# An attention kernel's products with v: six key tiles at a time, after two turns of scores in a row

## The chip, the cores and the metric

The kernel runs on one core of a Trainium2 chip. The metric is the device time of one execution in microseconds (us). Three executions of the kernel before took 3902.34, 3902.94 and 3906.36 us; their median, 3902.94 us, is the time before. The profiled execution has a span of 3893.8 us, and times read from the profile refer to that span.

## The reference

The kernel computes four layers one after the other on an image of 48 x 48 positions with 768 channels: a vision-transformer block, a Fourier mixing layer, a scan with a small convolution, and a second Fourier layer. The change touches only the attention inside the first layer. Cut to that part:

```python
# 12 heads of 64 channels, 2304 tokens (48 x 48)
attn = einsum('bqc,bkc->bqk', q * scale, k)
rel_h = einsum('bhwc,hkc->bhwk', r_q, Rh)     # position terms, per query
rel_w = einsum('bhwc,wkc->bhwk', r_q, Rw)
attn = softmax(attn + rel_h + rel_w, axis=-1)
out = einsum('bqk,bkc->bqc', attn, v)
```

All data is f32, except that the position terms are held in bf16.

## The kernel before, in words

The stages follow each other: layer norm with the q, k and v projections, attention, the output projection, the two layers of the MLP, then the other three layers. Attention is `attention_bounded` (L523). It works on pairs of heads: six pairs (`pr`), each with its 2 x 64 channels on the 128 partitions. The queries are cut into six chunks of 384 (`qc`), the keys into 18 tiles of 128 (`kt`). Scores are held with the keys on the partitions and the queries along the row, so that the product with v needs no transpose. Since the scores are known to be bounded, the exponential is taken with no maximum subtracted, and the sum over the keys is divided out at the end.

For one key tile there are four steps:

- `products` (L551): for each of the two heads one f32 matmul, keys times queries, 64 rows deep. The two heads use the upper and the lower half of the array's rows. The result fills a two-bank tile `s` in PSUM; the pool `at_ps` has three of them[...].
- `scores` (L559): for each head a bf16 matmul with a one-hot matrix (L564) adds the position terms to the same tile. ScalarE then takes the exponential of both heads at once (L566) into a tile `p` of SBUF from the pool `at_p`, and VectorE adds `p` to the running sum `acc` (L571, L574).
- `values` (L578): for each head one f32 matmul (L585), v times `p`, with 64 result rows. The two heads use the left and the right half of the array's columns, and add up over all 18 key tiles in one PSUM tile `av`.
- at the end of a chunk `row_sums` (L587) adds `acc` over the partitions with two matmuls (L592) and takes the reciprocal, and `finish` (L597) multiplies.

The loop at L604 runs over 216 turns (`work`, 36 chunks of six turns); a turn is `KB` = 3 key tiles of one chunk. In turn i the loop writes down `products` for its three tiles, then `scores` for them, and then `values` for the three tiles of the turn before. So a product with v never waits for its own exponentials: those of a turn run while TensorE does the products with v of the turn before it.

This is the order in which the program is written; a scheduler then gives each engine its own order. It takes instructions by priority, which is the order of writing, but may take a later one first where it reckons that the earlier one is not ready. Each engine works through its own list in order.

Beside attention, `weight_sums` (L735) prepares sums of weight blocks for later stages on GpSimd. It is advanced by one step every seven turns (L605), and takes the tiles through which it loads from the same pool `at_p` as the exponentials (L603).

Of the kernel before, what the change touches and what calls it, by code (L numbers as in the profile page):

```python
# [522 lines left out]
def attention_bounded(tc, ahead, oT, beside):  # L523

    nc = tc.nc
    QB = TB
    KB = 3
    (load_keys_values, load_chunk), kvs, qbs, ones, oneh = ahead
    with (
        tc.tile_pool(name="at_p", bufs=10) as pp,  # L540
        tc.tile_pool(name="at_r", bufs=2) as rp,
        tc.tile_pool(name="at_o", bufs=2) as op,
        tc.tile_pool(name="at_ps", bufs=3, space=PSUM) as ps_s,
        tc.tile_pool(name="at_pv", bufs=1, space=PSUM) as ps_v,
    ):
        keys = [kv[:, :T] for kv in kvs]
        vals = [kv[:, T:].rearrange("p (t c) -> p t c", t=NT) for kv in kvs]

        probs, scs = {}, {}

        def products(c, kt):  # L551
            pr, qc = c
            ps = ps_s.tile([P, 2, 512], F32, tag="s", name=f"s_{pr}_{qc}_{kt}")
            for s in range(2):
                rows = slice(s * HD, (s + 1) * HD)
                nc.tensor.matmul(ps[:, s, :QB], lhsT=keys[pr % 2][rows, kt * P : (kt + 1) * P], rhs=qbs[qc % 2][0][rows], start=True, stop=False)  # L556
            scs[c, kt] = ps

        def scores(c, kt):  # L559
            pr, qc = c  # L560
            b, j = divmod(kt, KJ)
            ps = scs.pop((c, kt))
            for s in range(2):
                nc.tensor.matmul(ps[:, s, :QB], lhsT=oneh[:NBR, b % 3, :], rhs=qbs[qc % 2][1][:NBR, s, b // 3, j, :], start=False, stop=True)  # L564
            p = pp.tile([P, 2, QB], F32, tag="p", name=f"p_{pr}_{qc}_{kt}")
            nc.scalar.activation(p, ps[:, :, :QB], AF.Exp)  # L566
            probs[c, kt] = p

            if kt == 1:
                acc = rp.tile([P, 2, QB], F32, tag="acc", name=f"acc_{pr}_{qc}")  # L570
                nc.vector.tensor_tensor(acc, probs[c, 0], p, ALU.add)  # L571
                probs[c] = acc
            elif kt > 1:
                nc.vector.tensor_tensor(probs[c], probs[c], p, ALU.add)  # L574

        avs, recs = {}, {}

        def values(c, kt):  # L578
            pr, qc = c
            if kt == 0:  # L580
                avs[c] = ps_v.tile([P, 512], F32, tag="av", name=f"av_{pr}_{qc}")
            p = probs.pop((c, kt))
            for s in range(2):
                rows = slice(s * HD, (s + 1) * HD)
                nc.tensor.matmul(avs[c][rows, :QB], lhsT=vals[pr % 2][:, kt, rows], rhs=p[:, s, :], start=kt == 0, stop=kt == NT - 1)  # L585

        def row_sums(c):  # L587
            pr, qc = c
            acc = probs.pop(c)
            rs = ps_v.tile([P, 512], F32, tag="rs", name=f"rs_{pr}_{qc}")  # L590
            for s in range(2):
                nc.tensor.matmul(rs[s * HD : (s + 1) * HD, :QB], lhsT=ones, rhs=acc[:, s, :], start=True, stop=True)  # L592
            rec = rp.tile([P, QB], F32, tag="rec", name=f"rec_{pr}_{qc}")
            nc.vector.reciprocal(rec, rs[:, :QB])
            recs[c] = rec

        def finish(c):  # L597
            pr, qc = c
            av, rec = avs.pop(c), recs.pop(c)
            nc.vector.tensor_tensor(oT[:, pr, qc * QB : (qc + 1) * QB], av[:, :QB], rec, ALU.mult)  # L600

        work = [((pr, qc), k0) for pr in range(NC) for qc in range(T // QB) for k0 in range(0, NT, KB)]
        other = beside(op, lambda name: pp.tile([P, 2, QB], F32, tag="p", name=name))  # L603
        for i in range(len(work) + 1):  # L604
            if i % 7 == 3:  # L605
                next(other, None)
            if i < len(work):
                c, k0 = work[i]
                pr, qc = c
                if k0 == 0:  # L610
                    nxt = (pr, qc + 1) if qc + 1 < T // QB else (pr + 1, 0)
                    if nxt[0] < NC:
                        load_chunk(qbs[nxt[1] % 2], nxt)
                    if qc == 1 and pr + 1 < NC:
                        load_keys_values(kvs[(pr + 1) % 2], pr + 1)
                for kt in range(k0, k0 + KB):
                    products(c, kt)
                for kt in range(k0, k0 + KB):
                    scores(c, kt)
            if i:  # L620
                c, k0 = work[i - 1]
                if k0 + KB == NT:
                    row_sums(c)
                for kt in range(k0, k0 + KB):
                    values(c, kt)
                if k0 + KB == NT:
                    finish(c)
        for _ in other:
            pass
# [627 lines left out]
def block_kernel(ctx: ExitStack, tc: tile.TileContext, a: dict):  # L1257
# [52 lines left out]
    with tc.If(bounded > 0) as which:  # L1310
        attention_bounded(tc, ahead, oT, beside)
# [387 lines left out]
```

## Time and profile before

| what | value |
|---|---|
| time, median of three | 3902.94 us |
| span of the profiled execution | 3893.8 us |
| TensorE matmul (PE) busy | 3755.5 us, 96% |
| TensorE weight loads (PEld) busy | 2283.2 us, 59% |
| VectorE (DVE) busy | 2050.0 us, 53% |
| ScalarE (ACT) busy | 1141.6 us, 29% |
| GpSimd (POOL) busy | 654.2 us, 17% |
| attention, first to last of its matmuls | 513.5 to 1690.1 us |
| in it: PE, DVE, ACT, POOL busy | 1171.5, 718.0, 480.1, 140.4 us |

PE stands for the matmuls and PEld for the weight loads, which overlap with them. Matmuls are pipelined: each is shown for about 0.48 us, while the next may start after 0.32 us. So a single duration of PE says little, and the distance between starts, or the busy time of a group divided by its count, says what one costs. In a line of the groups the fields are: source line, engine, operation, what it writes and reads, shapes, count; then the busy time of the group in us and the mean of one in ns; then the idle time of the engine just before the group's instructions, and what ended it. In a line of the timeline they are: start in us, length in us, engine, source line, operation, shapes and how many follow each other, and in brackets the idle time before.

In attention the granted clock of TensorE is 1.00 throughout.

### The profile page before, as it was taken

The page shows a single profiled execution, that of the slowest core. Times are in us where ns is not written, and L with a number is a line of the kernel's source. Part 1 is how long each engine was busy: PE and PEld are TensorE (multiplying, and loading weights), DVE is VectorE, ACT ScalarE, POOL GpSimd, SP SyncE. Part 2 cuts the span into 40 slices and gives each one's busy share as a digit, 9 for nine tenths or more (in the row PEclk, how much of TensorE's full clock was granted, in tenths as well). Part 3 has the DMA queues.
Part 4 walks back from the last instruction along what each step waited for, and adds up shares of the span by engine and source line. Part 5 has one row for each costly group of instructions (what it writes and reads, how often), then busy time and mean ns, then how long its engine had stood idle before and what let it go on. Part 6 is the DMA issues. An engine that isn't in the chain of part 4 may idle for free.

```text
span 3893.8 us, 54463 instructions
## 1 busy us (share of the span) xinstructions
PE 3755.5 (96%) x22018; PEld 2283.2 (59%) x22018; DVE 2050.0 (53%) x3185; ACT 1141.6 (29%) x1907; POOL 654.2 (17%) x496
## 2 busy tenths in 40 slices
PE   8999989999999999989999999999979998999998
PEld 4666544444444444445555555555558876996685
DVE  6655456666666666545425233232335358995445
ACT  1322244444444444411310120021013246223341
POOL 3101011111111111024000000000023210981131
PEclk9999999999999999999999999999989789999999
DMA  7656563424232322134335434533443312110434
GB/s 256 212 186 199 177 182 95 132 88 131 96 98 89 98 89 73 30 114 161 118 106 161 151 102 123 155 111 109 142 116 98 95 36 96 35 37 23 145 98 167
DMA packets 266954, 460.43 MB, mean 118 GB/s; under 512 B 33005, under 2 KB 219365, under 8 KB 260327
## 3 DMA queue, kind: packets, MB, share of 16 engines
q1 hardware_dynamic: 257063, 436.23, 36.4%
q10 hardware_dynamic: 9632, 20.65, 1.4%
q8 instruction: 175, 2.87, 0.3%
q14 instruction: 84, 0.69, 0.1%
HBM read 318.49 MB, written 138.31 MB: 117 GB/s over the span
## 4 chain that ended last, share of the span: by engine, by line
PE 87%; DVE 5%; DMA 4%; ACT 2%; issue 1%; SPq 1%; POOL 1%; ACTq 0%; DVEq 0%; POOLq 0%
PE p L860 13%; PE p L923 13%; PE s L556 11%; PE av L585 11%; PE qk L294 6%; PE s L564 6%; PE c L1076 4%; PE v L163 3%; PE pj L163 2%; PE f_z L1447 2%; PE f_z L1448 2%; PE f_x L1412 2%; PE f_u L1462 2%; PE so L1237 2%; PE f_w L1549 2%; DVE s L1186 2%
## 5 line engine op out<-in xcount | busy, mean ns | idle before, releaser
L574 DVE TENSOR_TENSOR acc<-acc,p 128x768 f32<-128x768 f32 x576 | 581.8, 1010 | 354.1 <-ACT p L566 315.9
L566 ACT ACTIVATE p<-s 128x768 f32<-128x768 f32 x648 | 478.4, 811 | 688.7 <-PE s L564 578.9
L923 PE MATMUL p<-w,h 128*128 128x384 f32 x1512 | 492.7, 486 | 0.0
L556 PE MATMUL s<-qt,kv 64*128 64x384 f32 x2592 | 477.7, 501 | 8.4 <-ACT p L566 4.7
L585 PE MATMUL av<-p,kv 128*64 128x384 f32 x2592 | 464.5, 493 | 0.0
L923 PEld LDWEIGHTS p<-w,h 128*128 128x128 f32 x1512 | 286.3, 190 | 196.7
L556 PEld LDWEIGHTS s<-qt,kv 64*128 64x128 f32 x2592 | 232.7, 186 | 248.8 <-ACT p L566 113.8
L585 PEld LDWEIGHTS av<-p,kv 128*64 128x64 f32 x2592 | 170.0, 136 | 225.2 <-issue 215.9
L860 PE MATMUL p<-x2nT,w 128*128 128x384 f32 x864 | 293.2, 489 | 3.9 <-POOL rr L899 3.9
L294 PE MATMUL qk<-xnT,wqk 128*128 128x384 f32 x756 | 251.5, 489 | 5.6 <-DMA wqk<-wqk_d 5.6
L1166 PE MATMUL c<-H,bands 128*48 128x96 f32 x5632 | 242.1, 247 | 11.7 <-issue 11.5
L564 PE MATMUL s<-bt,oneh 120*128 120x384 bf16 x1296 | 248.8, 328 | 0.0
L1166 PEld LDWEIGHTS c<-H,bands 128*48 128x48 f32 x5632 | 234.1, 123 | 19.8 <-issue 11.9
L860 PEld LDWEIGHTS p<-x2nT,w 128*128 128x128 f32 x864 | 165.2, 191 | 119.4 <-POOL rr L899 4.1
L860 PE MATMUL p<-xT,w 128*128 128x384 f32 x648 | 220.8, 486 | 0.0
L564 PEld LDWEIGHTS <-oneh 120*128 120x128 bf16 x1296 | 109.3, 98 | 174.5 <-issue 115.4
L294 PEld LDWEIGHTS qk<-xnT,wqk 128*128 128x128 f32 x756 | 144.2, 192 | 99.7 <-issue 7.9
L899 POOL TENSOR_TENSOR rr<-rr,ml_b 128x1152 f32<-128x1152 f32 x12 | 32.1, 2675 | 955.0 <-DMA rr<-xr_d 861.6
L855 ACT ACTIVATE h<-h,ml_b 128x384 f32<-128x384 f32 x144 | 88.3, 614 | 345.9 <-DVE h L875 174.3
L1174 POOL TENSOR_TENSOR t<-s,c 128x768 f32<-128x768 f32 x80 | 144.7, 1835 | 171.9 <-DVE s L1136 160.8
L860 PEld LDWEIGHTS p<-xT,w 128*128 128x128 f32 x648 | 123.2, 190 | 85.8
L1076 PE MATMUL c<-wsc,x2T 128*112 128x357 f32 (+1 forms) x576 | 151.6, 426 | 2.0 <-DVE c L1037 2.0
(312 smaller groups left out, 4763.5 us busy)
## 6 DMA issues: line engine op xcount, KB each, us to landing
w<-w1s_d SPq DMA_DIRECT2D x36, 768.0 KB
w<-w2s_d SPq DMA_DIRECT2D x36, 768.0 KB
bt<-rh_d SPq DMA_DIRECT2D x144, 162.0 KB
w<-w1s_d SPq DMA_DIRECT2D x36, 576.0 KB
w<-in_mlp_w_dram SPq DMA_DIRECT2D x27, 768.0 KB
wqk<-wqk_d SPq DMA_DIRECT2D x12, 1344.0 KB
yu<-f_ys SPq DMA_DIRECT2D x24, 672.0 KB
f_gt<-yu SPq DMA_DIRECT2D x24, 672.0 KB
```

Of the source, the lines that this page charges most:

```text
L163: nc.tensor.matmul(p[:, :TB], lhsT=rhs[n][:, c, t * P : (t + 1) * P], rhs=w[:, c, :], start=c == 0, stop=c == NC2 - 1)
L294: nc.tensor.matmul(p[:, :TB], lhsT=w[:, n, c, :], rhs=ops[sb][n][:, c, :], start=c == 0, stop=c == NC2 - 1)
L556: nc.tensor.matmul(ps[:, s, :QB], lhsT=keys[pr % 2][rows, kt * P : (kt + 1) * P], rhs=qbs[qc % 2][0][rows], start=True, stop=False)
L564: nc.tensor.matmul(ps[:, s, :QB], lhsT=oneh[:NBR, b % 3, :], rhs=qbs[qc % 2][1][:NBR, s, b // 3, j, :], start=False, stop=True)
L566: nc.scalar.activation(p, ps[:, :, :QB], AF.Exp)
L574: nc.vector.tensor_tensor(probs[c], probs[c], p, ALU.add)
L585: nc.tensor.matmul(avs[c][rows, :QB], lhsT=vals[pr % 2][:, kt, rows], rhs=p[:, s, :], start=kt == 0, stop=kt == NT - 1)
L860: nc.tensor.matmul(p[:, :TB], lhsT=w[n][:, c, :], rhs=rhs[n][:, c, :], start=c == 0, stop=c == NC2 - 1)
L923: nc.tensor.matmul(ps[t][:, :TB], lhsT=hs[left, f][:, t * P : (t + 1) * P], rhs=wt[:, f % KW2, :], start=f == 0, stop=f == NF2 - 1)
L1076: nc.tensor.matmul(ps[:K, i, :n], lhsT=xT[:, cc, tok : tok + K], rhs=w[:, cc, c0 : c0 + n], start=cc == 0, stop=cc == NC - 1)
L1166: nc.tensor.matmul(ps[r0 : r0 + G, k // 4, cols], lhsT=bands[:, n - GC, i, :] if gr else bands0[:, n, i, :], rhs=H[:, n, :, d : d + NPR], ...
L1174: GP.tensor_tensor(t, sc[:, ch], c1[:, m0 : m0 + GC].unsqueeze(2).to_broadcast([P, GC, RR, NPR]), ALU.mult)
```

## The change

The products with v are no longer written after every turn, but after every second one, and then for the six key tiles of the two turns before. Two turns of `products` and `scores` so follow each other with no `values` written between them. Since the number of turns in a chunk is even, a burst of six always belongs to one chunk. More tiles of exponentials are then alive at once, up to nine instead of six, so the pool `at_p` gets 13 buffers instead of 10. The purpose is that TensorE passes less often from one kind of product to another. What is computed, and the number of every kind of instruction, stay the same.

```diff
@@ attention_bounded
-        tc.tile_pool(name="at_p", bufs=10) as pp,
+        tc.tile_pool(name="at_p", bufs=13) as pp,
...
-            if i:
+            if i and i % 2 == 0:
                 c, k0 = work[i - 1]
                 if k0 + KB == NT:
                     row_sums(c)
-                for kt in range(k0, k0 + KB):
+                for kt in range(k0 - KB, k0 + KB):
                     values(c, kt)
                 if k0 + KB == NT:
                     finish(c)
```

## The prediction

> **What bounds the kernel now.** I began with the page's busy shares: PE 96% of the span, the next engine 53%. The chain of work that ended last says the same, and says how much of it is the attention this change touches:
>
> ```profile
> PE 87%; DVE 5%; DMA 4%; ACT 2%; issue 1%; SPq 1%; POOL 1%; ACTq 0%; DVEq 0%; POOLq 0%
> ```
>
> Its line for attention (L556, L564, L585) gives 11%, 6% and 11% of 3893.8 us. So I went to the groups of instructions, where the product lines stand with their counts, and a full-array line for comparison:
>
> ```profile
> L574 DVE TENSOR_TENSOR acc<-acc,p 128x768 f32<-128x768 f32 x576 | 581.8, 1010 | 354.1 <-ACT p L566 315.9
> L566 ACT ACTIVATE p<-s 128x768 f32<-128x768 f32 x648 | 478.4, 811 | 688.7 <-PE s L564 578.9
> L923 PE MATMUL p<-w,h 128*128 128x384 f32 x1512 | 492.7, 486 | 0.0
> L556 PE MATMUL s<-qt,kv 64*128 64x384 f32 x2592 | 477.7, 501 | 8.4 <-ACT p L566 4.7
> L585 PE MATMUL av<-p,kv 128*64 128x384 f32 x2592 | 464.5, 493 | 0.0
> L564 PE MATMUL s<-bt,oneh 120*128 120x384 bf16 x1296 | 248.8, 328 | 0.0
> ```
>
> Two readings. PE loses 8.4 us to waits in the whole attention; ACT and DVE wait for PE and not the reverse. And the busy time divided by the count: L585 464.5/2592 = 179 ns a pass, while L923, which fills the array, takes 492.7/1512 = 326 ns for the same 384 columns of f32. An f32 product is two passes (2592 passes for 1296 products), and the two heads' passes of L585 run side by side on the two column halves. A lone pass costs 326 ns, not 179.
>
> One turn (three key tiles) in order of time, PE alone:
>
> ```profile
> 902.15 2.21 PE L556 MATMUL s<-qt,kv 64*128 64x384 f32 x12
> 904.29 1.15 PE L564 MATMUL s<-bt,oneh 120*128 120x384 bf16 x6
> 905.37 2.16 PE L585 MATMUL av<-p,kv 128*64 128x384 f32 x12
> 907.46 0.92 PE L556 MATMUL s<-qt,kv 64*128 64x384 f32 x4
> ```
>
> Starts give the turn: products with k 2.14, bias 1.08, products with v 2.09, together 5.31 us. 216 turns x 5.3 us, plus 36 row sums of 0.70, are 1170 of the attention's 1177 us (513.5 to 1690.1). The weight loads of the same burst show its rhythm:
>
> ```profile
> 905.37 0.20 PEld L585 LDWEIGHTS av<-p,kv 128*64 128x64 f32 x4 [0.32 <-issue]
> 905.75 0.14 PEld L585 LDWEIGHTS av<-p,kv 128*64 128x64 f32 x2 [0.18 <-issue]
> 906.07 0.14 PEld L585 LDWEIGHTS av<-p,kv 128*64 128x64 f32 x2 [0.18 <-issue]
> 906.39 0.14 PEld L585 LDWEIGHTS av<-p,kv 128*64 128x64 f32 x2 [0.18 <-issue]
> 906.72 0.14 PEld L585 LDWEIGHTS av<-p,kv 128*64 128x64 f32 x2 [0.18 <-issue]
> ```
>
> Loads come two at a time, one per head, each 0.322 us after the last. A burst of six products is six such slots: 6 x 0.3225 = 1.935 us, and the other 0.15 of its 2.09 us is the switch: about 0.05 for the first weight load and 0.10 for the change to the next kind of product.
>
> **What the Trainium skill says.** "TensorEngine Tiling (Array Packing)", Key Properties: changing the tiling mode drains TensorE, while different tiles load and multiply in parallel. The trace agrees with both (0.15 us a burst; two loads per slot). "TensorE: Matmul & The Clock Gate", What overlaps and what doesn't: matmuls start and end strictly in program order. So a product with v that stands ahead of the next products with k is not overtaken; no trace here contradicts it. The same page, Measured speedup vs the span model, gives a packed group the time of one matmul plus about 4 ns a tile; here the slot of a pair equals L923's lone slot (0.32 us), so splitting a pair makes two slots of one.
>
> **What the change does to the order.** From the source I would expect, per two turns, k-products and bias twice and then twelve products with v. The built program differs, and its order on PE is what the chip runs. With P for products with k, S for bias, V for products with v, each with its number of products, it reads (steady state; row sums left out):
>
> ```
> before: P6 S6 V6    P6 S6 V6
> after:  P6 S6 V1    P6 S6 V11
> ```
>
> 107 times the scheduler puts one product (head 0 of the burst's first tile) between the two turns, and the burst starts with head 1 of that tile. Sums agree: 107 x 12 plus 12 in the last bursts = 1296 = 2592/2.
>
> **Part by part.**
> (1) Kinds of product change as often as before: six switches per two turns in both orders. The saving that a burst of six tiles could bring is therefore zero.
> (2) V1 has no partner. Its two passes take two slots alone: 2 x 0.3225 = 0.645 us plus its switch. V11 holds head 0 of five tiles and head 1 of six, so head 1's half sets its length: 6 x 2 = 12 slots, the same as twelve paired products. Per two turns V slots go from 12 to 14: +0.645 us, all on the path, since PE has nothing idle to put it in. 107 x 0.645 = +69.0 us. Lower bound: V1 with one weight load spared the 0.05 us of the first load, 0.593 x 107 = 63.5. Upper bound: a lone slot at the 326 ns of L923 and another 0.05 us of switch, about 0.70 x 107 = 75. I take 69, since the first pass waits for its weights either way.
> (3) The new wait: the second turn's P needs the score buffers (three) that the first turn's exponentials read. In the trace the exponentials begin at 904.83, 2.68 us after P starts, and are 0.70 apart:
>
> ```profile
> 904.83 2.21 ACT L566 ACTIVATE p<-s 128x768 f32<-128x768 f32 x3 [3.09 <-PE s L564]
> ```
>
> They end 3.49, 4.19 and 4.89 us after that P. The second P starts at 2.14 + 1.08 + 0.79 (V1 and its switch) = 4.01; its three tiles start two slots apart, with 0.1 us more after the first weight load: 4.01, 4.76 and 5.40. Each finds its buffer free by 0.5 us, so the wait costs nothing; behind it would stand S, V11 and all of PE, so 0.1 us of it would be 11 us in all.
> (4) ACT has 2.21 and DVE 3.08 us of work per turn (three exponentials; three sums). The shorter gap between turns is now 4.0 us, so neither becomes the bound. Row sums, where a chunk ends, come after the second turn's bias, at 4.01 + 2.14 + 1.08 = 7.23; the last of the sums they read (begun about 0.8 us behind the exponentials, 3.08 long) ends near 6.7: hidden.
> (5) Buffers 10 to 13: nine tiles of exponentials are alive instead of six, so four stay for the weight sums beside attention, as before. That sharing costs one stall in the trace:
>
> ```profile
> 548.99 2.21 ACT L566 ACTIVATE p<-s 128x768 f32<-128x768 f32 x3 [8.14 <-POOL pw0p L130]
> 549.85 1.62 PE L556 MATMUL s<-qt,kv 64*128 64x384 f32 x8 [3.21 <-ACT p L566]
> ```
>
> With 13 buffers that slot is first reused one turn later (the first exponential of the second chunk), over 5 us after; POOL is done by then. -3.2 us.
> (6) SyncE's queue moves a few weight loads behind bias loads; both are prefetched a chunk or more ahead (32 us), nothing.
> Sum: 3902.9 + 69.0 - 3.2 = 3968.7 us.
>
> **Rivals.**
> A, the lone product is free: its slots fall into time that the array loses anyway. Then only (5) is left, 3899.7; and if a V switch went as well (0.15 x 107 = 16) 3884. For it: the loader is idle 0.32 us ahead of each burst. Against: that gap is half of V1's slots, and the switch is not removed. Chance 0.06.
> B, the order as in the source: one switch less per two turns (-16), but the second P would come at 3.22 and wait for the first exponential until 3.49 plus about 0.05 for the signal: 0.32 x 107 = +34. 3902.9 - 16 + 34 - 3 = 3918. Against: the built order. Chance 0.04.
> C, V11 does not pair: every burst before starts with head 0, this one with head 1. If its 11 products ran singly, 22 slots instead of 12: 3.2 us x 107 more, 4314. For it: no trace has such a burst. Against: pairing here looks like two halves that each work off their own products. Chance 0.05.
>
> **How the numbers follow.** Main case 0.85: 3968.7, from 3963 to 3975 by the bounds of (2). The range widens these by ten-odd us for a stall that comes back (3.2 us each) or 0.1 us of the wait in (3): 3951 to 3987. A, B and C stay outside it. Faster by over 0.2% is the further half of A and a margin, 0.05; same 0.03; slower 0.92.
>
> **What would show it.** Right: attention (first L556 to last L585) longer by 62 to 72 us and everything after it unchanged; L585's busy time up by about 69 us with 2592 passes still; between two turns a group of L585 x2 of about 0.8 us, then a group of x22 of about 4.0; L556 still with a few us of idle on ACT. Wrong: L556 idle on exponentials of tens of us (B), an L585 group of x22 lasting 7 us (C), or groups of x2 that don't lengthen the two turns beyond 10.6 us (A).

## The result, and the profile after

| | before | changed |
|---|---|---|
| time, median | 3903.28 us | 3964.84 us |
| span of the profiled execution | 3893.8 us | 3964.2 us |
| attention, first to last of its matmuls | 1176.6 us | 1239.3 us (514.4 to 1753.7) |
| PE busy in the span | 3755.5 us | 3827.0 us |

The changed kernel is slower: the ratio is 1.0158, with a 95% interval from 1.0141 to 1.0176. In the two profiled executions attention takes 62.7 us more, and the medians of the time differ by 61.6 us. The spans of the profiled executions differ by 70.4 us; most of the rest, 6.9 us, lies after attention (2203.7 and 2210.6 us). In the nine traces of this document that stretch, which no edit touches, lasts between 2201 and 2212 us, so this is scatter and not the change.

The chain of work that ended last, by engine:

```profile
PE 89%; DVE 4%; DMA 3%; ACT 1%; issue 1%; POOL 0%; SPq 0%; ACTq 0%; DVEq 0%; POOLq 0%
```

PE's share rises from 87% to 89%; what came on top lies on PE. The groups of instructions that answer to those shown of before (after the bar: busy us, mean ns, idle before):

```profile
L574 DVE TENSOR_TENSOR acc<-acc,p 128x768 f32<-128x768 f32 x576 | 576.3, 1001 | 448.3 <-ACT p L566 409.6
L566 ACT ACTIVATE p<-s 128x768 f32<-128x768 f32 x648 | 478.5, 811 | 752.7 <-PE s L564 676.6
L585 PE MATMUL av<-p,kv 128*64 128x384 f32 x2592 | 532.4, 491 | 0.0
L923 PE MATMUL p<-w,h 128*128 128x384 f32 x1512 | 492.7, 486 | 0.0
L556 PE MATMUL s<-qt,kv 64*128 64x384 f32 x2592 | 476.5, 500 | 5.2 <-DVE rest_w L371 3.4
L564 PE MATMUL s<-bt,oneh 120*128 120x384 bf16 x1296 | 248.2, 328 | 0.0
```

Of the groups on PE shown here, the products with v (L585) are the only one that grew: 532.4 us busy instead of 464.5, with the same 2592 passes, nearly the same mean duration (491 and 493 ns) and no idle time before them. The others are as they were, to about 1 us. A group that costs 68 us more with equal instructions and no wait is one whose instructions overlap less.

The same stretch of two turns on PE, from the timeline:

```profile
908.80 2.21 PE L556 MATMUL s<-qt,kv 64*128 64x384 f32 x12
910.94 1.15 PE L564 MATMUL s<-bt,oneh 120*128 120x384 bf16 x6
912.02 0.86 PE L585 MATMUL av<-p,kv 128*64 128x384 f32 x2
912.81 2.21 PE L556 MATMUL s<-qt,kv 64*128 64x384 f32 x12
914.95 1.15 PE L564 MATMUL s<-bt,oneh 120*128 120x384 bf16 x6
916.03 4.08 PE L585 MATMUL av<-p,kv 128*64 128x384 f32 x22
920.04 0.59 PE L556 MATMUL s<-qt,kv 64*128 64x384 f32 x2
```

The two passes of the lone product (x2) hold the array from 912.02 to 912.81, 0.79 us, and the burst of 22 passes takes 4.01 us, which is what 24 passes in pairs would take. Two turns last 920.04 - 908.80 = 11.24 us instead of 10.61, which is twice the 5.303 us of the kernel before. Each kind of work on PE goes straight into the next; no bracket with an idle time stands at any of these lines.

### The profile page after: what moved, and what is told of

It reads as the page before. It is cut to its first block, busy times and chain, and to the rows that moved or that the text cites. A ratio compares the mean times of both kernels' runs of the same rounds, so it can differ in the third digit from the quotient of the medians.

```text
span 3964.2 us, 54473 instructions
## 1 busy us (share of the span) xinstructions
PE 3827.0 (97%) x22018; PEld 2315.1 (58%) x22018; DVE 2050.4 (52%) x3185; ACT 1141.9 (29%) x1907; POOL 645.3 (16%) x496
## 4 chain that ended last, share of the span: by engine, by line
PE 89%; DVE 4%; DMA 3%; ACT 1%; issue 1%; POOL 0%; SPq 0%; ACTq 0%; DVEq 0%; POOLq 0%
PE av L585 13%; PE p L860 12%; PE p L923 12%; PE s L556 12%; PE s L564 6%; PE qk L294 6%; PE c L1076 4%; PE pj L163 3%; PE v L163 3%; PE f_x L1412 2%; PE f_z L1447 2%; PE f_z L1448 2%; PE f_u L1462 2%; PE so L1237 2%; PE c L1166 2%; PE f_w L1549 2%
## 5 line engine op out<-in xcount | busy, mean ns | idle before, releaser
L585 PE MATMUL av<-p,kv 128*64 128x384 f32 x2592 | 532.4, 491 | 0.0
L556 PE MATMUL s<-qt,kv 64*128 64x384 f32 x2592 | 476.5, 500 | 5.2 <-DVE rest_w L371 3.4
L556 PEld LDWEIGHTS s<-qt,kv 64*128 64x128 f32 x2592 | 232.3, 186 | 245.2 <-issue 67.6
L585 PEld LDWEIGHTS av<-p,kv 128*64 128x64 f32 x2592 | 198.7, 137 | 264.3 <-issue 264.2
```

## The experiments

The first four were timed beside the same runs of the kernel before, the last three beside another set of such runs. Line numbers shift by one or more where an edit adds lines; the tile names show what a line is. In the diffs `last[0]` is the last bias matmul written so far, and `tc.issue_after` keeps TensorE's work in its block behind it; `values` takes the heads to do where only one is meant. P, S and V are used as in the prediction.

### One part alone: 13 buffers

```diff
-        tc.tile_pool(name="at_p", bufs=10) as pp,
+        tc.tile_pool(name="at_p", bufs=13) as pp,
```

> The kernel before with 13 buffers of exponentials and nothing else changed. Theory (buffers only remove the one stall on a weight-sum tile near the start): the 3.2 us of PE idle before the products with k at 549.85 are gone, attention 1173.4 us instead of 1176.6, time 3900.0 us. Rival (more buffers let the scheduler or the queues move something that costs): 3905 us or more.

Measured: 3898.53 us, ratio 0.9984 (0.9976 to 0.9992), attention 1172.9 us. The group of products with k, in the lines of attention alone:

```profile
L556 PE MATMUL s<-qt,kv 64*128 64x384 f32 x2592 | 477.8, 501 | 5.0 <-DVE rest_w L371 3.4 <-ACT p L566 1.6
```

The idle time before L556 falls from 8.4 to 5.0 us. What follows: the larger pool costs nothing and takes away one stall. The loss must lie in the new order.

### The same two turns with a pair ahead instead of a lone product

Against the changed kernel: the burst's first key tile is written after the odd turns, both heads, and held behind the last bias product, so that the scheduler cannot take half of it:

```diff
-            if i and i % 2 == 0:
+            if i % 2:
+                c, k0 = work[i - 1]
+                with tc.issue_after(last[0].ins):
+                    values(c, k0)
+            elif i:
                 c, k0 = work[i - 1]
                 if k0 + KB == NT:
                     row_sums(c)
-                for kt in range(k0 - KB, k0 + KB):
-                    values(c, kt)
+                with tc.issue_after(last[0].ins):
+                    for kt in range(k0 - KB + 1, k0 + KB):
+                        values(c, kt)
```

> The changed kernel with both heads of the burst's first key tile between the two turns instead of one: P6 S6 V2 P6 S6 V10. The number of switches and the early start of the burst are the same as in the changed kernel; only the pairing of that tile's two products differs. Theory (the cost is the missing partner): V slots per two turns 2 + 10 = 12 as before, time 3900 us (before, less the stall), attention 1173 us. Rival (the cost is that the burst is taken apart, whatever stands in front): time stays at 3940 to 3965 us.

Measured: 3899.65 us, ratio 0.9987 (0.9981 to 0.9994), attention 1174.6 us. On PE:

```profile
914.52 1.15 PE L565 MATMUL s<-bt,oneh 120*128 120x384 bf16 x6
915.60 0.87 PE L586 MATMUL av<-p,kv 128*64 128x384 f32 x4
916.40 2.21 PE L557 MATMUL s<-qt,kv 64*128 64x384 f32 x12
918.53 1.15 PE L565 MATMUL s<-bt,oneh 120*128 120x384 bf16 x6
```

The visit of four passes lasts 915.60 to 916.40, 0.80 us: the same as the changed kernel's visit of two passes (0.79). The second head's product came along for nothing, and the burst behind it shrank from 4.01 to 3.38 us. (3.38 us is the median of its 107 bursts.) One product moved by one place is worth about 65 us. This is the comparison that settles the cause: order of visits, number of switches and buffers are those of the changed kernel. The hold behind the bias products, which is new here, is no rival: the next kernel has it too, and there the cost is larger and not gone.

### Two lone products

Against the changed kernel: head 0 of the burst's first two key tiles stands between the turns; in the burst, head 1 of these is then set beside head 0 of the tiles two further on, so that all that can pair does:

```diff
+            if i % 2:
+                c, k0 = work[i - 1]
+                with tc.issue_after(last[0].ins):
+                    for kt in range(k0, k0 + 2):
+                        values(c, kt, (0,))
...
-                for kt in range(k0 - KB, k0 + KB):
-                    values(c, kt)
+                with tc.issue_after(last[0].ins):
+                    for n in range(2 * KB):
+                        values(c, k0 - KB + n, (1,))
+                        if n + 2 < 2 * KB:
+                            values(c, k0 - KB + n + 2, (0,))
```

> The changed kernel with two lone products between the two turns, head 0 of the burst's first two key tiles; the burst then takes head 1 of these tiles paired with head 0 of later ones: four pairs and two lone products of head 1. Theory (each lone product costs the slots in which it has no partner): V slots per two turns 4 + 12 = 16 instead of 14 in the changed kernel and 12 before, 0.645 us more each, 107 times: 69 us over the changed kernel, 4034 us. Rival (the cost belongs to the visit, not to the number of lone products): 3965 us.

Measured: 4038.74 us, ratio 1.0337 (1.0320 to 1.0354), attention 1310.1 us, 70.8 us over the changed kernel. On PE:

```profile
911.29 1.50 PE L586 MATMUL av<-p,kv 128*64 128x384 f32 x4
912.73 2.21 PE L557 MATMUL s<-qt,kv 64*128 64x384 f32 x12
```

Four passes as with the pair ahead, but all of one head: 911.29 to 912.73, 1.44 us instead of 0.80. Each further lone product costs its two slots, and the visit as such nothing more.

### The order as written: nothing between the two turns

Against the changed kernel, the whole burst is held behind the second turn's bias products:

```diff
-                for kt in range(k0 - KB, k0 + KB):
-                    values(c, kt)
+                with tc.issue_after(last[0].ins):
+                    for kt in range(k0 - KB, k0 + KB):
+                        values(c, kt)
```

> The changed kernel with the products with v of a burst held behind the last bias product written before them, so that no lone product stands between the two turns: P6 S6 P6 S6 V12. Theory (the lone product costs two unpaired slots, 0.645 us each time): these 69 us go; one switch less per two turns saves 0.15 x 107 = 16 us; the second turn's products with k now wait about 0.32 us for the first exponential, 34 us in all. Time about 3918 us, attention about 1191 us, V22 and V2 groups replaced by V24 of 4.02 us, L556 idle on ACT about 35 us. Rival (long bursts as such are slow, or holding more exponentials is): time stays near 3965 us. Rival (the wait is larger than thought, the second and third tile wait too): 3940 us or more with over 55 us of idle on ACT.

Measured: 3935.65 us, ratio 1.0071 (1.0054 to 1.0088), attention 1211.0 us. On PE:

```profile
906.56 2.21 PE L557 MATMUL s<-qt,kv 64*128 64x384 f32 x12
908.70 1.15 PE L565 MATMUL s<-bt,oneh 120*128 120x384 bf16 x6
910.09 2.32 PE L557 MATMUL s<-qt,kv 64*128 64x384 f32 x12 [0.25 <-ACT p L567]
912.35 1.15 PE L565 MATMUL s<-bt,oneh 120*128 120x384 bf16 x6
913.43 4.09 PE L586 MATMUL av<-p,kv 128*64 128x384 f32 x24
917.45 2.21 PE L557 MATMUL s<-qt,kv 64*128 64x384 f32 x12
```

The lone product is gone, and the time falls by 29 us, but less than I expected, by 18 us. The second turn's products with k start 1.39 us after the bias instead of 1.08, as forecast (0.32 later), but then also take 2.26 us to the next bias instead of 2.14: the second and third tile each lose some 0.06 us as well. That this too comes from the exponentials is shown only by the next pair of runs. In sum, over two turns, 2.14 + 1.40 + 2.25 + 1.08 + 4.02 = 10.89 us against 10.61, that is 0.28 x 107 = 30 us; I had reckoned 18. Against 13 buffers alone, attention is 38.1 us longer. The other 8 us lie at the start: some 6 are the stall on a weight-sum tile, which in this order came back, with the slow clock behind it, and 1.6 are a slow clock from 521.7 to 525.0 (0.50). The window behind the stall, with the busy time of PE, PEld, DVE, ACT and POOL, and last the granted clock, the DMA share and GB/s:

```profile
552.90:558.90 6.00, 5.94 (x18) 2.24 (x20) 1.69 (x2) 2.22 (x4) 1.77 (x2) 0.50 0.49 177
```

In the stall an exponential waited 2.8 us for a weight-sum tile, PE idled 2.7 us, and for the next 6 us the clock stood at 0.50.

### The same without the wait, and its control

Both kernels take exponentials and sums of the first half of the queries only and set the rest to 1.0, so half of the output is not the attention's. TensorE's work is not touched.

```diff
-            nc.scalar.activation(p, ps[:, :, :QB], AF.Exp)
+            nc.scalar.activation(p[:, :, : QB // 2], ps[:, :, : QB // 2], AF.Exp)
+            nc.vector.memset(p[:, :, QB // 2 :], 1.0)
```

The control, on the order of before with 13 buffers:

> A control for the next run: the kernel before with 13 buffers, and exponentials and sums of only the first half of the 384 queries; the other half of each tile of exponentials and of the sum is set to 1.0 by VectorE. So the output of half of the queries is not the attention's. TensorE's work is the same to the instruction. Theory (ScalarE and VectorE are off the path here): same time as with 13 buffers alone, 3898 us, attention 1173 us.

Measured: 3900.87 us, ratio 0.9992 (0.9981 to 1.0002), attention 1175.0 us.

The order as written:

> The kernel in which no product with v stands between the two turns (P6 S6 P6 S6 V12), with exponentials and sums of only the first half of the queries, the rest set to 1.0, as in the control. An exponential takes about 0.45 us instead of 0.81, so the first ends about 1.0 us after the bias products begin, before the second turn's products with k could start at 1.08. Theory (the second turn waited for its buffers, and that is all that this order lost): the step from bias to products with k falls from 1.40 to about 1.08 us and the second P from 2.25 to 2.14; one switch less per two turns leaves 10.46 us per two turns instead of 10.61: 16 us under the control, 3882 us. Rival (the direct change from bias to products with k, or the long burst, costs what the switch saves): no less than the control, 3898 us.

Measured: 3885.70 us, ratio 0.9952 (0.9936 to 0.9967), attention 1162.4 us. On PE:

```profile
912.16 2.21 PE L557 MATMUL s<-qt,kv 64*128 64x384 f32 x12
914.30 1.15 PE L565 MATMUL s<-bt,oneh 120*128 120x384 bf16 x6
915.38 2.21 PE L557 MATMUL s<-qt,kv 64*128 64x384 f32 x12
917.52 1.15 PE L565 MATMUL s<-bt,oneh 120*128 120x384 bf16 x6
918.59 2.80 PE L589 MATMUL av<-p,kv 128*64 128x384 f32 x16
```

Now 1.08 us pass from bias to products with k, and 2.14 from these to bias: both waits are gone (an exponential takes 0.49 us here), and the time is 15 us under the control (16 expected). In the two traces attention differs by 12.6 us: two turns take 10.46 us instead of 10.61, which makes 16 us over 107, but both have the stall near the start, and it costs about 3.3 us more in this order. So the saving that the change was made for exists, 0.15 us for each visit to the products with v that is left out, and with exponentials at their real length of 0.81 us the three score buffers take back nearly three times as much (0.32 + 0.11 us).

### Heads apart

The kernel before, with the six products of each burst sorted by head:

```diff
-                for kt in range(k0, k0 + KB):
-                    values(c, kt)
+                for s in range(2):
+                    for kt in range(k0, k0 + KB):
+                        values(c, kt, (s,))
```

> The kernel before with the six products with v of each turn in another order: head 0 of the three tiles, then head 1 of the three, instead of both heads tile by tile. Same instructions, same number of switches. Theory A (the two halves of the array each work off their own products, whatever stands between them in the program): still six slots a burst, 2.09 us, time 3903 us. Theory B (a product only pairs with its neighbour in the program, apart from one pass at the border): eleven or twelve slots instead of six, 1.6 to 1.9 us more for each of 216 bursts, 345 to 415 us in all, 4250 to 4320 us.

Measured: 4052.47 us, ratio 1.0385 (1.0363 to 1.0408), attention 1323.2 us. Neither theory: a burst takes 2.78 us, eight slots, not six and not eleven. The weight loads of one burst:

```profile
904.93 0.19 PEld L585 LDWEIGHTS av<-p,kv 128*64 128x64 f32 x2 [0.32 <-issue]
905.31 0.14 PEld L585 LDWEIGHTS av<-p,kv 128*64 128x64 f32 x1 [0.18 <-issue]
905.63 0.84 PEld L585 LDWEIGHTS av<-p,kv 128*64 128x64 f32 x7 [0.19 <-issue]
906.66 0.14 PEld L585 LDWEIGHTS av<-p,kv 128*64 128x64 f32 x1 [0.19 <-issue]
906.98 0.14 PEld L585 LDWEIGHTS av<-p,kv 128*64 128x64 f32 x1 [0.18 <-issue]
```

For two slots the loads come singly, then in pairs, then singly again. The starts of the single matmuls form two rows of six passes: 904.93, 905.31, 905.63, 905.95, 906.28, 906.60 and 905.64, 906.01, 906.33, 906.66, 906.98, 907.30. In the built program too, and not only in the source, head 0's three products stand ahead of head 1's, so the second row must be head 1's: it begins when head 0's first product is done, while head 0's third (906.28) has not begun. So a half of the array takes work past the other half's products, but only a little way: past one that has not begun, and not, at 904.93, past two. The numbers fit one product running and one waiting for each half, with a third blocking what stands behind it; no run here tests that picture further.

## Why the prediction was right

The forecast was 3968.7 us and the measured time is 3964.84, inside the range of 3951 to 3987. By its steps:

1. **The same number of switches.** Right. The phases of the changed kernel start as the forecast laid them out: P 2.14, S 1.08, V1 0.79, P 2.14, S 1.08, V11 4.01 us.
2. **The lone product.** Right in kind and size. All visits to the products with v together take 512.4 us; before, without its one stall, 444.6: 67.8 us against the 69.0 of the sum. Shown by the pair put in its place (the cost goes) and by the second lone product (it doubles), and not only by the trace.
3. **No wait for the score buffers.** Right: L556 idles 5.2 us in the whole of attention, 3.4 of them at its start. The exponentials of the stretch above begin at 911.48, 2.68 us after P, and the second P comes at 4.01, as worked out:

```profile
911.48 2.21 ACT L566 ACTIVATE p<-s 128x768 f32<-128x768 f32 x3 [4.97 <-PE s L564]
```

4. **ACT, DVE and row sums hidden.** Right; row sums follow the bias after 1.08 us, as in before.
5. **One stall less, -3.2 us.** About right in size (13 buffers alone took 3.7 us off attention), wrong in its reason. I had written that GpSimd "is done by then". It is not: the exponentials one turn later still wait for it,

```profile
550.65 2.21 ACT L566 ACTIVATE p<-s 128x768 f32<-128x768 f32 x3 [3.75 <-POOL pw0p L130]
```

which is 1.95 us later than 548.70, when they would otherwise begin (2.68 us after their P at 546.02). But row sums and a burst of 4 us stood behind them on PE, and the wait ended inside these. In this order the stall was hidden, not removed, and that it fell where it cost nothing was luck; in the order as written, where it fell at another place, it cost about 6 us. With 13 buffers alone no exponential waits for GpSimd.
6. **SyncE's queue.** Right, nothing to be seen.

What remains between 65.8 us forecast and 62.7 us in attention is 1.2 us in step 2, 0.5 us in step 5, and 1.4 us at the entry. There the clock in the trace of before was not 1.00, as I had it, but 0.50 from 514.5 to 517.8; in the trace of the changed kernel it was 1.00 in the same stretch. The order has no part in this last piece that a run here shows.

Of the rivals, A fell with the pair and the two lone products: the slots are not free. B was not the order that was built, so it could not come true here; for its own order it had the right shape and was too low: it took only the first tile's wait (0.32 us) and missed 0.11 us for the later ones and the stall that came back. C fell in the changed kernel's own trace: the burst that begins with head 1 takes 4.01 us, so all of it but its last product pairs. And where I leaned on the strict order of matmuls ("TensorE: Matmul & The Clock Gate", What overlaps and what doesn't), the lone product was indeed not overtaken by the products with k (912.02 and 912.81 above); but between the two column halves heads apart shows starts that are out of program order (head 1's first at 905.64, head 0's third at 906.28). There the measurement decides.

## What to carry to other kernels

Where two half-array matmuls share a slot, a product's price is nothing or all of its slots (two, 0.645 us, for these), depending on whether one for the other half stands close behind it. So check in the built order, and not in the source, that a scheduler keeps the pair together: here it took just one of the two ahead, 107 times. That it did so to fill the gap before the second turn's products with k is likely, but no run here shows it. Grouping work to save switches (0.15 us a visit here) pays only if the buffers that the grouping makes scarcer come free in time: here three PSUM tiles and exponentials of 0.81 us cost 0.43 us per group. The best versions that ran, 13 buffers alone (0.9984) and the pair ahead (0.9987), owe their small gain, as far as the traces show it, to the stall that is gone in the one and hidden in the other, and not to the grouping.

## What the runs showed of the hardware that I had not expected

- Sorting the products by head cost 0.70 us a burst, two slots and a first weight load: each half of the array takes its work past one product of the other half that has not begun, and not past two.
- After 2.7 us without a matmul the clock stood at 0.50 for some 6 us (order as written, at 552.9), while in the kernel before 3.2 us of idle time at 546.6 left it at 1.00 in the window from 549.8 to 555. So an idle time of this length may or may not cost a second time; what decides it is not shown here.
